# Reordering a planned instruction stream: a later landing time for transposed planes, a preferred sum, a moved row addition (four-layer graph network, one core)

## The chip, the cores and the metric

The kernel runs on one core of one Trainium2 chip. The metric is device time in microseconds (us); lower is better. Three runs of the kernel before took 2829.81, 2833.12 and 2834.18 us, median 2833.12. One further execution was profiled.

In the profile, PE is TensorE's matmul, PEld its weight load, DVE is VectorE, ACT is ScalarE, POOL is GpSimd and SP is SyncE, which only issues DMAs. "out<-in" names what an instruction writes and reads, and "x4" counts instructions.

## The reference

The input x has 128 graphs of 64 nodes with 512 features, float32. Four layers follow one another, each h = relu(layernorm(x)) and then x = x + f(h):

- layers 0, 1 and 3: q, k, v = h Wq, h Wk, h Wv; attention with 8 heads of 64 inside each graph of 64 nodes, masked by one 64 x 64 adjacency matrix, with a softmax; layers 1 and 3 then multiply by an output matrix, and layer 3 also adds a layer norm of the result to it;
- layer 2: rel = (h Wq)(h Wk)^T inside a graph, multiplied by the adjacency matrix, each row divided by its norm, then rel (h Wv), without a softmax.

Every projection is a product of 8192 x 512 by 512 x 512. All arithmetic is in float32.

## The kernel before

**Tiles.** The 8192 rows are cut into 16 tiles of 512 rows (8 graphs), so there are 64 steps n = 0 to 63, layer l = n // 16. A tile of step n is held transposed as `hT`. x lives in DRAM between the layers, one tensor for each of them (`x_0`, `x_1`, ..., `out_dram`).

**Products.** A projection (`projection`, L644) is a Strassen-Winograd product: 7 products of half-size blocks, each one bank of PSUM and 1.73 us of TensorE (8 matmuls of 128x256, started 216 ns apart). Their operands are `hT` itself and `S`, sums of its quarters, or `SO` for the output projections. In layers 1 to 3 one of the seven is cut a second time ("finer"): its 7 small products come as two groups, "4a" and "4b", in the same bank. After 4a, ScalarE copies two quarters (`q<-mm`, z5) and VectorE adds `q` ("u2"); 4b must wait for that. After 4b `close_2` (L633) makes the last quarter of the result on POOL and VectorE. Product 7 ends with the sum "Y22" of `u3` and `z5`, which POOL makes for nearly all projections (`qT<-u,z`, `kT<-u,z`, `v<-u,z`, about 1.3 us each). The order of the seven is a list: `ORDER`, `FINER`, and `LAST_V` for the very last v.

**Planes.** A tile is transposed by DMA (`turn`, L516). VectorE, or ScalarE for the attention's weights, splits the float32 values into two 16-bit planes (`z<-xin`, `z<-s`). SP issues a transposing DMA (`hp<-z`). ScalarE joins the planes (`hT<-hp`, `s<-hp`):

```python
split(zp, src.bitcast(U16).rearrange("p (f w) -> p w f", w=2))
plan.sync.dma_start(
    hp.rearrange("p w c t -> p (w c) t"), zp.rearrange("p w f -> p (w f)"), transpose=True
)
act.copy(dst.bitcast(U16).rearrange("p c (t w) -> p w c t", w=2), hp)
```

POOL then makes `S` from `hT` (`sums_x`, L571). The attention (`attend`, L830) takes the scores (`s<-mm,mask` and the maxima `mx` on VectorE, the shift `s<-s,mx` on POOL), the exponential on ScalarE, the sums `sr` and the scaling, and then transposes `s` in the same way.

**Layer 2.** It has two projections, with the folded weight Wq^T Wk (`a2`) and with Wv (`v2`). `relate` (L1043) makes the relation, its norms `ss` and the factor `rn`, and VectorE's evacuations `xo` of the values use `rn`.

**Additions to x.** `adds` (L1016) adds to a tile of x in DRAM with an accumulating DMA of 1 MB, issued by POOL: either a result, or a constant row (the bias of layer 1, or `bet` of layer 3) spread over the tile (`x<-row`, `out_dram<-row`). The first row of layers 1 and 3 (steps 16 and 48) is put into a queue of generators, which comes forward by one tick with each product of a projection:

```python
if l in (1, 3) and k == 0:
    spawn(adds(n), 16)
```

**The order.** No instruction is issued while this program runs through the layers. `Plan.record` (L95) notes each as a step with its engine, what it depends on, how long it takes (`busy`) and how long after that its result is there (`late`), both from formulas. `Plan.order` (L156) then plays the steps through on a model of the five engines: whichever engine is free next takes, of its ready steps, the one of the lowest rank. The rank is the place in which the step was recorded, less `RUSH` = 100 for a step that reads PSUM and for one in `plan.hot` (the POOL steps of `close_2` are). `Plan.issue` (L229) issues the steps in the order of their planned starts, so every engine gets a fixed sequence, and all instructions have the line L233. On the chip each engine then takes its sequence in order and waits on semaphores. For DMAs the model holds a time `moved` at which SP's transfers are through, and another (`added`) for POOL's:

```python
elif e == "sync":
    moved = max(moved, at + 1400) + late / (170 if calls[0][2].get("transpose") else 280)
    late = moved + 600 - at - busy
```

Times in the model are in ns. One clock of the generators' queue is one product.

Of the kernel before, what the change touches and what calls it, by code (L numbers as in the profile page):

```python
# [46 lines left out]
LAST_V = (1, 6, "4a", 5, 7, "4b", 2, 3)  # L47
# [11 lines left out]
class Plan:  # L59
# [60 lines left out]
    def add(self, eng, calls, reads, writes, busy, late):  # L120
# [8 lines left out]
        if eng == "tensor":  # L129
            self.products.append(i)  # L130
        elif calls[0][0] == "dma_start" and len(self.products) >= AHEAD:
            deps.add(self.products[-AHEAD])
            if eng == "gpsimd":
# [22 lines left out]
    def order(self):  # L156
        n = len(self.steps)
        wait = [0] * n
        users = [[] for _ in range(n)]
        for i, s in enumerate(self.steps):  # L160
            lags = {**self.lags.get(i, {}), **{d: 0.0 for d in s[2]}}
            wait[i] = len(lags)
            for d, lag in lags.items():
                users[d].append((i, lag))


        rank = [
            i - (n if i in self.front else 0)
            - RUSH * (i in self.hot or any(
                v.tensor.name.startswith("mm_") for c in s[1] for v in c[1][1:] if isinstance(v, bass.AP)  # L170
            ))
            for i, s in enumerate(self.steps)
        ]
        ready = [0.0] * n
        free = {e: 0.0 for e in ("tensor", "vector", "scalar", "gpsimd", "sync")}
        added = 0.0
        moved = 0.0
        port = 0.0
        soon = {e: [] for e in free}
        here = {e: [] for e in free}  # L180
        for i in range(n):
            if not wait[i]:
                heapq.heappush(soon[self.steps[i][0]], (0.0, rank[i], i))
        out = []
        while len(out) < n:
            best = None
            for e in free:
                while soon[e] and soon[e][0][0] <= free[e]:
                    heapq.heappush(here[e], heapq.heappop(soon[e])[1:])
                if here[e]:  # L190
                    at = free[e]
                elif soon[e]:
                    at = soon[e][0][0]
                else:
                    continue
                if best is None or at < best[0]:
                    best = (at, e)
            at, e = best
            if not here[e]:
                while soon[e] and soon[e][0][0] <= at:  # L200
                    heapq.heappush(here[e], heapq.heappop(soon[e])[1:])
            i = heapq.heappop(here[e])[1]
            eng, calls, _, busy, late = self.steps[i]
            moves = calls[0][0] == "dma_start"
            if e == "gpsimd":
                busy += max(0.0, port - at)
            if moves and e == "gpsimd":
                moved = max(moved, at) + 8000
                added = max(added + 6000, at + 8500)
                late = added - at - busy  # L210
            elif e == "sync":
                moved = max(moved, at + 1400) + late / (170 if calls[0][2].get("transpose") else 280)
                late = moved + 600 - at - busy
            elif e == "vector" and late == PORT:
                busy += max(0.0, free["gpsimd"] - at)
                port = at + busy
            free[e] = at + busy
            out.append((at, i))
            for u, lag in users[i]:
                same = self.steps[u][0] == e  # L220
                ready[u] = max(ready[u], at + busy - lag + (0.0 if same and not moves else late))
                wait[u] -= 1
                if not wait[u]:
                    heapq.heappush(soon[self.steps[u][0]], (ready[u], rank[u], u))
        self.start = {i: at for at, i in out}
        self.span = max(free.values())
        return [i for _, i in sorted(out)]
# [47 lines left out]
LEVEL2 = {c + l for l in "13" for c in "qkvo"} | {"a2", "v2"}  # L275
RUSH = 100
WARM = 22
AHEAD = 16


# [37 lines left out]
def gnn_stack_kernel(  # L318
# [11 lines left out]
    plan = Plan(nc)  # L330
# [28 lines left out]
    pw = blocks(mm.take("pw"))  # L359
    for i in range(WARM):  # L360
        pe.transpose(pw[:, i % KC, :], ident, ident)
# [40 lines left out]
    def finer(name):  # L402
        return name in LEVEL2
# [123 lines left out]
    def layer_norm(n):  # L527
# [19 lines left out]
        if n == 0:  # L547
            for t in range(NT):
# [7 lines left out]
                if t == 1:  # L556
                    for i in range(WARM // 2):
                        pe.transpose(pw[:, i % KC, :], xins[n][0][:, ts(i % KC, P)], ident)
# [54 lines left out]
    def quarter(t, prod, i, j):  # L613
        u, v = (j, i) if prod is prod_T else (i, j)
        return t[:, u, v * P : (v + 1) * P]
# [11 lines left out]
    def shared_2(prod, q):  # L627


        i, j = (1, 2) if prod is prod_N else (2, 1)  # L630
        return q[:, 0], q[:, i], q[:, j], q[:, 3]
# [12 lines left out]
    def projection(prod, name, xop, nm, emit, order=None):  # L644
        w = W[name]
        order = order or (FINER if finer(name) else ORDER)

        banks, tmp = {}, {}

        def bank(i):  # L650
            banks[i] = mm.take(f"{i}_{nm}")
            return banks[i]

        def tmp_tile(tag):
            tmp[tag] = p1.tile([P, D], F32, tag=tag, name=f"{tag}_{nm}")
            return tmp[tag]

        X = {1: 1, 2: 1, 6: 6, 7: 6, 5: 5, 3: 5, 4: 4, "4a": "4a", "4b": "4a"}
        for i in order:
            home = X[i]  # L660
            first = home == i
            ps = bank(home) if first else banks[home]
            plan.begin()
            if i in BLOCKS:
                prod(ps, w[:, BLOCKS[i]], xop()[i], first)
            else:
                pv = ps.rearrange("p (u v) -> p u v", u=2)
                prod_2(prod, pv, name, xop(), (1, 5, 6, 4) if i == "4a" else (2, 7, 3))
            plan.end()
            if i == 1:  # L670
                act.copy(tmp_tile("s1"), ps)
            elif i == 2:
                emit("Y11", ps)
            elif i == 6:
                dve.tensor_tensor(tmp_tile("u2"), ps, tmp["s1"], ALU.add)
                emit("u2", tmp["u2"])
            elif i == 5:
                emit("z5", ps, tmp_tile("z5"))
            elif i == 7:
                dve.tensor_tensor(tmp_tile("u3"), ps, tmp["s1"], ALU.add)  # L680
                emit("u3", tmp["u3"])
                emit("Y22", tmp["u3"], tmp["z5"])
            elif i == 4:
                emit("Y21", ps, tmp["u3"])
            elif i == 3:
                emit("Y12", ps, tmp["u2"])
            elif i == "4a":
                q = p1.tile([P, 4, P], F32, tag="q", name=f"q_{nm}")
                q0, u2, u3, z5 = shared_2(prod, q)
                act.copy(q0, quarter(pv, prod, 0, 0))  # L690
                dst, base, mid, bias = emit("close")
                if bias is None:
                    act.copy(z5, quarter(pv, prod, 0, 1))
                else:
                    act.activation(z5, quarter(pv, prod, 0, 1), AF.Identity, bias=bias[1])
                dve.tensor_tensor(u2, quarter(pv, prod, 1, 1), q0, ALU.add)
            elif i == "4b":
                dve.tensor_tensor(u3, quarter(pv, prod, 1, 1), q0, ALU.add)
                dve.tensor_tensor(z5, z5, u3, ALU.add)
                if base is None:  # L700
                    t = tmp["u3"]
                    base = t.rearrange("p (u v) -> p u v", u=2)
                    mid = t[:, P : 3 * P].rearrange("p (u v) -> p u v", u=2)
                close_2(prod, pv, q, base, mid, dst, bias)
            if i in (2, 7, 3, 4, "4b"):
                mm.give(f"{home}_{nm}")
            if i != order[-1]:
                yield
# [307 lines left out]
    def adds(n, y=None):  # L1016
        if y is not None:
            add_out(n, y)
        for i in ROWS.get(n, (1,)) if y is not None else (0,):
            add_out(n + i, R["b1" if n < 2 * NB else "bet"].unsqueeze(1).to_broadcast([P, NT, D]))  # L1020
        yield
# [94 lines left out]
    def spawn(gen, delay=0):  # L1116
        heapq.heappush(queue, (clock[0] + delay, count[0], gen))
        count[0] += 1
# [73 lines left out]
    for n in range(N):  # L1192
# [13 lines left out]
        if n == 3 * NB:  # L1206
            spawn(relate(n), 5)
        if l in (1, 3) and k == 0:
            spawn(adds(n), 16)
        if l != 2:  # L1210
            qT = p1.tile([P, KC, T], F32, tag="qT", name=f"qT_{n}")
            q_emit = emit_bias(region_T(qT), (bqc0, bqc1)[l]) if l < 2 else emit_plain(region_T(qT))
# [45 lines left out]
    for t in range(NT):  # L1258
# [14 lines left out]
        at = slice(t, t + 1)  # L1273
# [41 lines left out]
```

## Time and profile before

| | |
|---|---|
| runs | 2829.81, 2833.12, 2834.18 us |
| profiled execution | 2833.51 us, of which its span (first to last instruction) 2831.7 |
| granted TensorE clock, mean | 0.998 |
| PE busy | 2809.0 us (99%), 26787 matmuls |
| VectorE, POOL, ScalarE busy | 67%, 67%, 53% |
| first product that has real input | at 8.04 us |
| layer 1 starts (n = 16), layer 2, layer 3 | near 700, 1560, 2000 us |
| `x<-row` on POOL, 1 MB each | 16, median 13.8 us to landing |
| `hT<-hp` copies on ScalarE | 252 of 1.353 us in the mean |

The page of the profile first gives the busy time of each engine, then groups of instructions. A wait of an engine is put down to the instruction whose semaphore came last. The chain is the path that ended last, followed back from the end of the program; a "DMA" piece in it is a transfer, "issue" is time in which nothing shows that the engine waited for. Matmuls are pipelined: their records overlap (379 ns each, started every 216 ns), so gaps between them are also read from start to start. The timeline lists an engine's instructions with start and duration, and in brackets how long the engine was idle before and for what.

### The profile page before, as it was taken

To read this page: it belongs to the slowest core of one execution; us is meant where nothing else is said; L and a number is where in the kernel's file an instruction comes from. 1 tells how busy PE (TensorE), PEld (TensorE's weight loads), DVE (VectorE), ACT (ScalarE), POOL (GpSimd) and SP (SyncE) were. 2 spreads that over 40 slices of the span, in tenths; PEclk is the share of its full clock that TensorE was granted. 3 is DMA by queue.
4 is the path that set the end of the run, shared out by engine and by line. 5 is a ranking of instruction groups with operands and counts; after the bars stand their busy time and mean duration, and the time that the engine had idled before them with its cause. 6 is when DMAs were issued, how large, how long until landed. Compare 5 with 4: busy or idle time off the path is not lost.

```text
span 2831.7 us, 65612 instructions
## 1 busy us (share of the span) xinstructions
PE 2809.0 (99%) x26787; PEld 2479.2 (88%) x26787; DVE 1885.2 (67%) x3505; ACT 1489.5 (53%) x2111; POOL 1884.1 (67%) x1849
## 2 busy tenths in 40 slices
PE   9999999999999999999999999999999999999998
PEld 8888788888888888888888888888888888888887
DVE  6666566665666656556656665666578778778777
ACT  5566647555564654645644444443545555555552
POOL 6555565557667666576579645556687887777875
PEclk9999999999999999999999999999999999999999
DMA  6666567556355564564565766565545664554644
GB/s 155 138 152 148 125 157 152 120 135 163 75 104 101 114 129 78 104 122 81 113 129 130 177 155 155 142 157 158 107 82 89 108 114 79 119 106 80 126 84 90
DMA packets 634446, 343.55 MB, mean 121 GB/s; under 512 B 484256, under 2 KB 565408, under 8 KB 634144
## 3 DMA queue, kind: packets, MB, share of 16 engines
q1 hardware_dynamic: 600880, 273.30, 42.5%
q0 software_dynamic: 33264, 66.06, 13.9%
q8 instruction: 209, 3.42, 0.5%
q14 instruction: 93, 0.76, 0.1%
HBM read 120.10 MB, written 102.76 MB: 79 GB/s over the span
## 4 chain that ended last, share of the span: by engine, by line
PE 93%; DVE 2%; DMA 2%; ACT 1%; POOL 1%; SPq 1%; issue 1%; POOLq 0%; DVEq 0%; ACTq 0%
PE mm L233 93%; SPq L233 1%; DVE xo L233 1%; DMA hp<-z 1%; POOL rn L233 0%; DMA xin<-x 0%; ACT s L233 0%; DVE z L233 0%; DMA xin<-in_x_dram 0%; DVE st L233 0%; ACT z L233 0%; POOL S L233 0%; ACT hT L233 0%; DVE u L233 0%; DMA xo<-in_x_dram 0%
## 5 line engine op out<-in xcount | busy, mean ns | idle before, releaser
L233 PE MATMUL mm<-S,w 128*128 128x256 f32 x3584 | 820.0, 380 | 0.6 <-DVE xo L233 0.6
L233 PEld LDWEIGHTS mm<-S,w 128*128 128x128 f32 x3584 | 670.2, 190 | 88.2 <-DVE xo L233 1.0
L233 PE MATMUL mm<-hT,w 128*128 128x256 f32 (+1 forms) x3040 | 618.7, 346 | 1.2 <-DVE q L233 1.0
L233 PEld LDWEIGHTS mm<-hT,w 128*128 128x128 f32 x3040 | 517.6, 190 | 62.0 <-DVE q L233 1.4
L233 DVE TENSOR_TENSOR u<-mm,s 128x512 f32<-128x512 f32 x414 | 283.9, 686 | 304.6 <-PE mm L233 224.4
L233 PE MATMUL mm<-w,S 128*128 128x256 f32 x2048 | 479.6, 382 | 0.7 <-issue 0.7
L233 PEld LDWEIGHTS mm<-w,S 128*128 128x128 f32 x2048 | 378.2, 190 | 52.8 <-issue 2.4
L233 ACT COPY hT<-hp 128x1024 uint16<-128x1024 uint16 x252 | 330.7, 1353 | 142.7 <-DMA hp<-z 142.0
L233 PE MATMUL mm<-w,hT 128*128 128x256 f32 (+1 forms) x1696 | 351.1, 347 | 7.3 <-DVE q L233 5.6
L233 PEld LDWEIGHTS mm<-w,hT 128*128 128x128 f32 x1696 | 293.0, 191 | 44.8 <-DVE q L233 9.2
L233 POOL TENSOR_TENSOR qT<-u,z 128x512 f32<-128x512 f32 x64 | 88.0, 1376 | 346.4 <-DVE u L233 329.0
L233 DVE COPY z<-xin 128x1024 uint16<-128x1024 uint16 x252 | 234.2, 950 | 47.2 <-ACT xin L233 39.2
L233 POOL TENSOR_TENSOR S<-hT 128x512 f32<-128x512 f32 x126 | 172.1, 1366 | 115.0 <-ACT hT L233 115.0
L233 ACT COPY s<-hp 128x1024 uint16<-128x1024 uint16 x188 | 243.8, 1350 | 7.1 <-DMA hp<-z 6.2
L233 POOL TENSOR_TENSOR s<-s,mx 128x1024 f32<-128x1024 f32 x96 | 184.9, 1967 | 70.5 <-DVE mx L233 70.5
L233 PE MATMUL mm<-w,SO 128*128 128x256 f32 x992 | 229.2, 379 | 0.0
L233 ACT ACTIVATE xin<-xin,nb,rs 128x512 f32<-128x512 f32 x256 | 195.3, 811 | 56.9 <-DVE nb L233 56.9
L233 ACT COPY s<-mm 128x512 f32<-128x512 f32 x211 | 122.6, 583 | 187.7 <-PE mm L233 109.4
L233 ACT COPY z<-s 128x1024 uint16<-128x1024 uint16 x188 | 189.6, 1047 | 37.0 <-POOL s L233 36.9
L233 PEld LDWEIGHTS mm<-w,SO 128*128 128x128 f32 x992 | 183.9, 190 | 22.6
L233 DVE BATCH_NORM_STATS2 st<-xin 128x6 f32<-128x512 f32 x256 | 171.8, 671 | 37.7 <-DMA xin<-x 18.8
L233 PE MATMUL mm<-w,oT 128*128 128x256 f32 (+1 forms) x994 | 189.6, 334 | 0.7 <-DVE q L233 0.3
(131 smaller groups left out, 4114.8 us busy)
## 6 DMA issues: line engine op xcount, KB each, us to landing
xin<-x SPq DMA_DIRECT2D x128, 256.0 KB, 3.7
xin<-in_x_dram SPq DMA_DIRECT2D x64, 256.0 KB, 3.9
x<-row POOLq DMA_DIRECT2D x16, 1024.0 KB, 13.8
x<-xo POOLq DMA_DIRECT2D x16, 1024.0 KB, 9.5
xin<-out_dram SPq DMA_DIRECT2D x64, 256.0 KB, 6.6
out_dram<-row POOLq DMA_DIRECT2D x16, 1024.0 KB, 16.6
out_dram<-xo POOLq DMA_DIRECT2D x15, 1024.0 KB, 12.4
out_dram<-xo SPq DMA_DIRECT2D x36, 256.0 KB, 2.5
```

The source lines that it names most:

```text
L233: getattr(getattr(self.nc, eng), op)(*a, **k)
```

## The change

Three edits, all of which act on the order alone; the recorded steps are the same.

```diff
@@ Plan.order
             elif e == "sync":
                 moved = max(moved, at + 1400) + late / (170 if calls[0][2].get("transpose") else 280)
-                late = moved + 600 - at - busy
+                late = moved + (MARGIN if calls[0][2].get("transpose") else 600) - at - busy
@@ constants
 RUSH = 100
 WARM = 22
+MARGIN = 2000
 AHEAD = 16
@@ projection, after product 7
                 emit("u3", tmp["u3"])
                 emit("Y22", tmp["u3"], tmp["z5"])
+                if order is not LAST_V:
+                    plan.hot.add(len(plan.steps) - 1)
@@ the loop over n
         if l in (1, 3) and k == 0:
-            spawn(adds(n), 16)
+            spawn(adds(n), 20)
```

In the model, the result of a transposing DMA is there 2000 ns after `moved` instead of 600. The step Y22 gets the rank of the steps that read PSUM, except in the last v. The first row addition of layers 1 and 3 is recorded four products later: at n = 16 POOL's instruction comes behind the shifts of the scores and the closing sums of v (n = 16), where it was behind the closing sums of kT. The planner's new order differs in many other places by a few instructions on each engine.

## The prediction

> **What bounds the kernel now.** I read the busy shares first, then what TensorE waited for, then the chain of waits at the two places that TensorE's idle time pointed to.
>
> ```profile
> PE 2809.0 (99%) x26787; PEld 2479.2 (88%) x26787; DVE 1885.2 (67%) x3505; ACT 1489.5 (53%) x2111; POOL 1884.1 (67%) x1849
> ```
>
> TensorE is busy for 2809.0 of 2831.7 us; no other engine passes 67%. The change adds no product and takes none away, so all it can move is the rest: some 8.0 us until the first real product (the chain has "8.04 377.42 PE mm"), 7.6 us after the last one (PE's work ends at 2824.1), and the waits between. These are few:
>
> ```profile
> PE mm L233 <- DVE q L233: 6.9, 4, 4.6
> PE mm L233 <- ACT xin L233: 2.6, 1, 2.6
> PE mm L233 <- POOL ident masks.py:199: 1.4, 1, 1.4
> PE mm L233 <- DVE s L233: 1.3, 1, 1.3
> ```
>
> The columns are total us, times, longest. The second and third rows are the start. The first holds one wait of 4.6 us; the chain around it reads:
>
> ```profile
> 705.44 2.58 DMA xin<-x
> 708.02 10.63 DMA hp<-z
> 718.65 0.02 issue
> 718.67 0.04 ACT hT L233
> 718.72 1.16 issue
> 719.87 0.42 ACT q L233 x2
> 720.29 0.02 issue
> 720.32 0.30 DVE q L233
> ```
>
> A transposed plane (hp<-z) took 10.63 us to land, where the two before it, issued at 704.11 and 706.07, took some 3.4. ScalarE's next instruction in its order was the copy of this plane, so two small copies of a product (q<-mm), which had nothing to do with the plane, ran behind it; VectorE's sum q and TensorE's "4b" came after them. The timeline shows what slowed the plane and how long ScalarE stood:
>
> ```profile
> 706.67 1.49 POOL L233 DMA_DIRECT2D x<-row  x1
> 718.67 1.33 ACT L233 COPY hT<-hp 128x1024 uint16<-128x1024 uint16 x1 [7.95 <-DMA hp<-z]
> ```
>
> The row is 1 MB, issued 1.35 us before the plane, and it landed 11.2 us later. After the gap the next 7 matmuls start 427 ns apart instead of 216: 7 x 0.211 = 1.48 us more. The place costs 4.60 + 0.16 (the start of the restarted one) + 1.48 = 6.2 us.
>
> The other waits, with what the restart adds, are one of 1.43 us at 1745 (sum s), 1.13 at 1557 and 1.18 at 1603 (q), 0.74 at 1999, 0.5 at 878, 0.3 at 1546, together 5.3; and in layer 2 six of 0.22 us (start to start), 57.1 us apart, from 1660.6 to 1947.8, too short for the view of waits, each of this form in the chain:
>
> ```profile
> 1829.58 1.65 POOL rn L233
> 1831.25 0.57 DVE xo L233 x2
> 1831.83 0.22 issue
> 1832.05 1.26 DVE xo L233 x3
> 1833.31 0.21 DVE q L233
> ```
>
> Five evacuations xo stand ahead of q on VectorE, and TensorE's 4b starts at 1833.56, 0.22 late. (The wait at 1603 is one period ahead of the first of them.)
>
> **What the Trainium skill says.** "DMA: Bandwidth & Descriptors", section "Issuing engines are not separate DMA queues": transfers of all queues run on the same 16 engines and interleave. The trace agrees: SP's plane 3.4 us alone, 10.63 beside POOL's row. "TensorE: Matmul & The Clock Gate", section "What's actually happening": the clock halves after an idle window of about 3.4 us. Agrees: only the 4.60 us gap shows the doubled cadence, 427 ns against 216. The same page, "Architectural detail": ScalarE and VectorE run strictly in order; the chain above is that. "SBUF — State Buffer", section "Who interferes with whom": some VectorE copies and GpSimd's instructions lock each other out for a whole instruction. Agrees: z<-xin takes 0.69 at best, up to 1.76 beside POOL, 0.95 in the mean.
>
> **The change part by part.** It changes only the order in which the recorded steps are issued: every engine keeps its instructions. Durations are from the profiled execution, 2833.51 us: span 2831.7 plus 1.8 around it. The runs' median is 2833.12, so 0.4 less.
>
> 1. *First row moved back (16 to 20 ticks), at n=16 and 48.* On POOL the DMA of n=16 now stands behind the shifts of both halves of the scores (s<-s,mx, 1.9 each) and the three closing sums of v, ahead of the four sums S (1.27 each). By then the four planes of the next tile have been issued on SP. So the plane lands in 3.4 us and the 6.2 us go. What is late next: the DMA's 1.49 us of POOL now stand straight before S. By the durations, the second sum ends near 722.6 on before's clock, and TensorE, no longer held, wants S near 721.4: 1.2 us lost (0 to 2.5). The row now overlaps the planes of the attention (s to hp) in place of those of hT; the last copy s<-hp would come near 729.7, about 0.7 us late for the products of the values (0 to 1.5). And v's own 4b keeps a VectorE with two maxima of 1.21 us about it: 0.2 (0 to 0.5). Net at n=16: -6.2 + 2.1 = -4.1; bounds -6.2 and -1.7. At n=48 (out<-row at 2002) TensorE never waited on planes, and the DMA goes behind the sums of a weight: nothing, 0 to +0.5 if S falls late there too.
>
> 2. *Margin: a transposed plane is taken to land 1.4 us later.* The planner puts small ScalarE work (the q and z5 copies, 0.2 to 0.6 us each) ahead of plane copies of 1.35 us. That shortens chains to TensorE; the price is that hT and S come up to 1.4 us later. The cover is there: S is ready 16 us ahead of its first product in layer 2 (1851.7 against 1868), 20 in layer 3 (2212.7 against 2232.2), the half SO 23. In layer 2 VectorE now has q behind four xo, not five, and POOL has rn ahead of rs: one xo of 0.39 us against a lack of 0.22. Six waits go: -1.3 (-1.3 to 0).
>
> 3. *Last quarter's sum (Y22, POOL, 1.38 us) preferred.* It now passes the quarter sums of S and the shifts of the scores, which then come 1.4 us later; the 16 to 23 us above hide that. POOL at 67% has room. Price nothing, up to +1 for values that wait on a later shift. LAST_V is left out of this, but the order of its products moves: 4b comes one product closer to the end, and the values after it wait on VectorE's and POOL's last sums of v: +0.5 (0 to 0.9) in the tail, the rest of which stays at 21.7 us.
>
> 4. *Everything else moves a little.* Of the 5.3 us of single waits, at least that at 1557 (q behind a z copy of 1.76) has its cause moved: z copies now follow q there. At 1745 the input is late by DMA (7.3 us) and stays. I take -1.0 (-4 to +3, since new ones of about 1 us can arise at any change of layer).
>
> Sum: -4.1 - 1.3 + 0 + 0.5 - 1.0 = -5.9, so 2833.1 - 5.9 = **2827.2 us**.
>
> **The rivals.** 0.2%, about what a measurement here can tell from no change, is 5.7 us.
>
> *A: the wait moves, it doesn't go.* The 1 MB row still needs 11 us somewhere, and POOL's in-order queue now puts it before S and beside the planes of the attention. For it: those planes also pass through ScalarE in order. Against: their products have others to run ahead of them. With the upper bound of step 1 (-1.7), layer 2 (-1.3), and the tail and other waits at +0.5 each: -2.0, 2831.1. If layer 2 too keeps its waits: 2832.4.
>
> *B: slower, since the second halves of the finer products start too soon.* In the new order 4b follows 4a after a single product of 1.73 us in 108 of some 158 places (before 90), the others have 3.46. Within 1.73 us ScalarE must copy q0 and z5 (0.42) and VectorE add q (0.30), with whatever its order puts ahead; one xo group and a z copy (0.95) fill it, as layer 2 shows now at 0.22 a place. At 0.22 x 108 = 23.8 the gain is gone and 18 lost. It decides from (5.9 + 5.7) / 0.22 = 53 of the 108 places on; with 58 it ends at 2827.2 + 12.8 = 2840. For it: VectorE is busy for 7 to 8 tenths in most slices of layer 3, 5 to 6 in earlier ones. Against: of before's 90 such places only the six of layer 2 and some four more waited, and the later plane copies clear ScalarE's way.
>
> *C: the order of the plan is not that of the chip*, so the margin does nothing and only step 1 counts: -4.1 + 0.5 = -3.6, 2829.5.
>
> **How the numbers follow.** The main case 0.72; A 0.08; C 0.04; B 0.16. Within the main case the sum spreads from about -9.5 to -3 (2823.6 to 2830), and I put 5 parts of 8 beyond -5.7, since the 5.3 us of single waits leave more room below than the +3 above: 0.45 of all, and 0.27 short of it. A and C fall within 0.2%, B beyond it. Faster 0.45, same 0.27 + 0.12 = 0.39, slower 0.16. The range reaches down to all single waits and the periodic ones gone, with step 1 at its lower bound (-6.2 - 1.3 - 5.3 + 0.5 = -12.3, so 2821), and up to B's 2840.
>
> **What would show it.** Right: no TensorE gap over 1 us near 720 and no run of 427 ns; hp<-z near 3.4 us for the fourth plane of n=17; the row's DMA after v's sums; waits for q down from 6.9 to under 2 us; no waits in layer 2 of period 57 us; PE's busy time within 2 us of 2809 and the whole gain in gaps. Wrong: a wait on S or s near 722 to 730 of over 3 us; many waits for q of 0.2 to 0.4 us in layers 1 to 3; or a hT copy on ScalarE that still stands behind a plane of 10 us with a q copy after it.

## The result: 2820.52 us, and the profile after

The changed kernel took 2820.52 us (median of five runs, 2818.44 to 2821.14), the kernel before 2832.04 in five runs: ratio 0.9958, 95% interval 0.9944 to 0.9973, so 11.5 us less. The forecast was 2827.2, in a range from 2821 to 2840. The sign was right; the size was about half of what came, and the time lies 0.5 us under the range.

The profiled execution took 2818.44 us, its span 2816.5. The page's busy line, and what TensorE waited for:

```profile
PE 2803.3 (100%) x26787; PEld 2476.3 (88%) x26787; DVE 1885.6 (67%) x3505; ACT 1494.9 (53%) x2111; POOL 1876.9 (67%) x1849
```

```profile
PE mm L233 <- POOL ident masks.py:199: 1.4, 1, 1.4
PE mm L233 <- ACT xin L233: 1.0, 1, 1.0
PE mm L233 <- ACT s L233: 0.7, 1, 0.7
...
PE mm L233 <- DVE q L233: 0.3, 1, 0.3
PE mm L233 <- POOL S L233: 0.2, 1, 0.2
```

The waits for q, 6.9 us before, are 0.3; the largest that are not the start are two of 0.7, one of them for a copy s<-mm of ScalarE that empties a bank. But PE's busy time fell too, by 5.7 us, with the same matmuls. "Busy" hides two things: matmuls at half clock, and the short waits inside a group of small matmuls, since the records overlap.

At n = 16 the timeline of POOL shows the row's DMA in its new place, behind the closing sums of v (the first of them is v's Y22):

```profile
712.94 1.28 POOL L233 TENSOR_TENSOR v<-u,z 128x512 f32<-128x512 f32 x1 [0.61 <-DVE u L233]
714.30 0.73 POOL L233 TENSOR_TENSOR u<-u,q 128x256 f32<-128x256 f32 x1
714.99 0.46 POOL L233 TENSOR_TENSOR v<-u,q 128x128 f32<-128x128 f32 x1
715.39 1.49 POOL L233 DMA_DIRECT2D x<-row  x1
716.42 1.77 POOL L233 TENSOR_TENSOR S<-hT 128x512 f32<-128x512 f32 x1
718.27 1.27 POOL L233 TENSOR_TENSOR S<-S,hT 128x512 f32<-128x512 f32 x1
```

And that of ScalarE its two q copies, ahead of the next planes; no small copy stands behind a late plane:

```profile
708.81 0.58 ACT L233 COPY z<-mm 128x512 f32<-128x512 f32 x1
709.28 0.44 ACT L233 COPY q<-mm 128x128 f32<-128x128 f32 x2
709.60 2.58 ACT L233 COPY hT<-hp 128x1024 uint16<-128x1024 uint16 x2
```

SP issued the last plane of the next tile at 709.58, and it landed within 4.3 us, since its copy starts at 713.89; the row comes 1.5 us after that. Layer 2 has lost its periodic waits: four xo, then q (the timeline of VectorE), and TensorE's 4b at 1820.26 follows the product before it without a gap.

```profile
1818.21 1.66 DVE L233 SCALAR_TENSOR_TENSOR xo<-mm,rn,xo 128x256 f32<-128x256 f32 x4 [1.33 <-POOL rn L233]
1819.79 0.28 DVE L233 TENSOR_TENSOR q<-mm,q 128x128 f32<-128x128 f32 x1
```

**An account by start times.** To see the hidden losses too, I took for each matmul the time from the start of the one before it, less the median for that pair of shapes, and summed what came to over 0.15 us at one place (the evenly repeated slow matmuls of layer 2's norms left out, which are the same in all kernels). In us of one profiled execution each:

| kernel | start | rest of layer 0 | 540 to 700 | n = 16 (700 to 760) | 760 to 1640 | 1640 to 2003 | layer 3 | tail | sum | time less sum |
|---|---|---|---|---|---|---|---|---|---|---|
| before | 5.8 | 0.3 | 2.7 | 6.5 | 3.5 | 4.3 | 1.2 | 1.2 | 25.6 | 2807.9 |
| after | 3.5 | 1.2 | 0 | 1.5 | 0.6 | 1.5 | 0 | 1.4 | 9.7 | 2808.8 |
| row_only | 4.0 | 3.1 | 1.9 | 7.5 | 3.0 | 2.8 | 1.1 | 1.2 | 24.6 | 2808.2 |
| margin_only | 4.5 | 0 | 0 | 6.7 | 0.5 | 1.5 | 4.9 | 5.8 | 23.8 | 2808.2 |
| hot_only | 5.7 | 5.2 | 2.1 | 8.6 | 0.2 | 3.1 | 0.3 | 1.4 | 26.6 | 2807.8 |
| move_dma | 6.1 | 1.5 | 0.2 | 4.1 | 3.5 | 3.8 | 0 | 1.2 | 20.3 | 2808.1 |
| swap_act | 4.6 | 1.2 | 2.5 | 6.3 | 3.5 | 3.8 | 0 | 1.2 | 23.0 | 2808.4 |
| after_dma_back | 3.5 | 4.9 | 0 | 7.2 | 0.6 | 0.3 | 0 | 1.4 | 17.9 | 2808.6 |
| margin_1300 | 6.0 | 0 | 0 | 1.1 | 0.8 | 4.4 | 0 | 1.4 | 13.7 | 2808.9 |
| margin_1700 | 3.5 | 1.9 | 0 | 7.0 | 1.0 | 0.7 | 6.9 | 4.1 | 25.0 | 2810.2 |
| margin_3000 | 3.5 | 2.2 | 0 | 1.0 | 1.4 | 0 | 10.7 | 3.6 | 22.2 | 2808.9 |
| after_dma_later | 5.6 | 1.0 | 0 | 9.7 | 0.6 | 0.6 | 0 | 1.4 | 18.8 | 2808.4 |
| row_24 | 3.8 | 1.6 | 0 | 2.2 | 0.6 | 0.6 | 5.4 | 1.4 | 15.6 | 2809.0 |
| margin_hot_k | 5.8 | 0.2 | 0 | 7.9 | 0 | 0.9 | 30.1 | 3.6 | 48.5 | 2808.2 |

The last column (the profiled execution's time less the sum) stays within 2807.8 to 2810.2, while the times lie 38 us apart: the account leaves little out. Each row is one execution, and parts of it are chance. All kernels begin with the same instructions, yet the first column spans 2.6 us: in the six executions with 5.6 to 6.1 the granted clock was halved at the start, in the eight with 3.5 to 4.6 it was not. Before, row_only, move_dma and swap_act share their order up to n = 16, and lose 2.7, 1.9, 0.2 and 2.5 from 540 to 700; the 1.2 of layer 3 before come in one more of these four. So part of the 15.1 us between the two profiled executions is no effect of the change; the medians, 11.5 us apart, bear the weight.

### The profile page after: what moved, and what is told of

It is laid out like the page before. It is cut to its first block, busy times and chain, and to the rows that moved or that the text cites. A ratio compares the mean times of both kernels' runs of the same rounds, so it can differ in the third digit from the quotient of the medians.

```text
span 2816.5 us, 65510 instructions
## 1 busy us (share of the span) xinstructions
PE 2803.3 (100%) x26787; PEld 2476.3 (88%) x26787; DVE 1885.6 (67%) x3505; ACT 1494.9 (53%) x2111; POOL 1876.9 (67%) x1849
## 4 chain that ended last, share of the span: by engine, by line
PE 96%; DVE 1%; DMA 1%; POOL 1%; SPq 1%; issue 0%; ACT 0%; POOLq 0%; DVEq 0%; ACTq 0%
PE mm L233 96%; SPq L233 1%; DMA xin<-x 0%; DMA xin<-in_x_dram 0%; POOL S L233 0%; DVE st L233 0%; DVE xo L233 0%; DMA hp<-z 0%; POOL xo L233 0%; DVE s L233 0%; DMA xo<-in_x_dram 0%; DVE u L233 0%; DVE z L233 0%; DVE kT L233 0%; DVE mx L233 0%
## 5 line engine op out<-in xcount | busy, mean ns | idle before, releaser
L233 DVE COPY z<-xin 128x1024 uint16<-128x1024 uint16 x252 | 219.1, 886 | 38.1 <-ACT xin L233 33.8
L233 POOL TENSOR_TENSOR S<-hT 128x512 f32<-128x512 f32 x126 | 162.0, 1286 | 65.3 <-ACT hT L233 65.3
L233 ACT ACTIVATE s<-s 128x1024 f32<-128x1024 f32 (+1 forms) x112 | 108.2, 968 | 169.3 <-DVE s L233 92.7
## 6 DMA issues: line engine op xcount, KB each, us to landing
out_dram<-xo POOLq DMA_DIRECT2D x15, 1024.0 KB, 10.6
```

The lines of the kernel that those rows point to most:

```text
L233: getattr(getattr(self.nc, eng), op)(*a, **k)
```

## The experiments

Each was timed in rounds against the kernel before on the same chip. The chips differ from one set of rounds to another, and the kernel before took 2832.04 to 2834.02 us in the median on them, so the ratios compare more closely than the times.

**The edits one at a time.** First the third edit: `spawn(adds(n), 20)` in the kernel before.

> The kernel before with the third edit alone (20 ticks for 16). Its order: TensorE's, ScalarE's and SP's sequences are those of before; on POOL the row's DMA of n=16 keeps its place, only that of n=48 moves by two instructions. Theory 1 (the edit does nothing by itself; the DMA at n=16 was moved by the other two edits together): the gap of 4.6 us at 720 stays, time within 1.5 us of the kernel before. Theory 2 (the prediction's step 1): 4.1 us less.

Measured: 2832.62 us, ratio 1.0002 (0.9994 to 1.0011). The edit alone does nothing, as theory 1 said. Nor does it add anything to the other two: compared instruction by instruction, all three edits give on every engine the sequence that the first two give without it. The DMA's new place is a joint effect of the other two edits on the planner.

Then the margin alone, the first edit:

> The kernel before with MARGIN = 2000 alone. The row's DMA of n=16 keeps its place ahead of the shifts, but ScalarE has the q copies ahead of the third and fourth copy of hT there. Theory 1 (what frees TensorE is the order on ScalarE): no gap of more than 2.5 us near 720, so 3 to 4 us from there, 1.5 from the periodic waits of layer 2, 3 from the waits at 1557, 1603 and 1999: 8 us less, 2824. Theory 2 (the prediction's steps 2 and 4; the gap at 720 needs the DMA moved): 2.3 us less.

Measured: 2831.55 us, ratio 0.9997 (0.9989 to 1.0006). Neither theory. What theory 1 wanted from 540 to 2003 did come: without n = 16 those columns hold 2.0 us where before had 10.5. It was given back, in layer 3 and the tail, 10.7 us against 2.4. The waits of TensorE:

```profile
PE mm L233 <- POOL S L233: 3.1, 1, 3.1
PE mm L233 <- ACT z L233: 2.1, 3, 1.1
...
PE mm L233 <- DVE v L233: 1.9, 1, 1.9
...
PE mm L233 <- DVE kT L233: 1.2, 2, 0.6
```

At n = 16 the wait is no longer for q but for S: ScalarE still stands 6.6 us for a plane there. In layer 3 the scores wait for kT at two places, 1.6 us by the account. The chain at one of them reads:

```profile
2403.38 2.97 POOL SO L233 x2
2406.35 0.41 POOL kT L233
2406.77 0.42 POOL oT L233
2407.19 0.07 issue
2407.26 1.29 POOL oT L233 x3
2408.54 1.23 POOL kT L233
```

Sums SO and their quarters (oT) stand on POOL ahead of the large kT sum of 1.23 us, which is Y22. That is the step that the second edit prefers. The other 9 us have several causes: copies of z behind the copy of a plane, a wait for the maxima mx, and in the tail four waits and the one for v.

The preferred Y22 alone, the second edit:

> The kernel before with the preferred Y22 alone. The row's DMA and the q copies behind the fourth plane stay at n=16. Theory 1: the gap near 720 stays; the slow starts of scores (kT,qT) in layer 0, 1.5 us in all between 583 and 666, go, since kT's sum comes sooner; layer 2's waits stay or change by chance: 1 to 2 us less. Theory 2 (the prediction's step 3): nothing, 0 to +1.

Measured: 2831.53 us, ratio 0.9993 (0.9985 to 1.0001). By the account the single waits from 760 to 1640 go, but n = 16 costs 8.6, and layer 2's periodic waits and the wait at 1999 stay. The gain at kT in layer 0 that theory 1 named did not show with this edit (2.1 us are left there, 0 with the margin; but see above how much of that is chance). This execution also shows one wait of 2.1 us near 154, for a plane of the attention; I did not pursue whether the order makes it.

So -0.7 and -0.7 alone, not told from none, but -11.5 together.

**The DMA by itself.** In the kernel before, one instruction moved after planning: the first row's DMA behind the first shift.

```diff
+    row = next(i for i in seq if plan.steps[i][0] == "gpsimd" and plan.steps[i][1][0][0] == "dma_start")
+    pool = [i for i in seq if plan.steps[i][0] == "gpsimd"]
+    behind = pool[pool.index(row) + 1]
+    seq.remove(row)
+    seq.insert(seq.index(behind) + 1, row)
```

> The kernel before with one instruction moved and nothing else: POOL's first row DMA stands behind the first shift s<-s,mx of n=16, not ahead of it, some 8 us later by the trace. Theory 1 (the DMA that slows the plane is the cause of the 6.2 us): the fourth plane lands in under 5 us, the gap near 720 goes, and the DMA's 1.5 us on POOL cost at most 1.2 us ahead of S: 4 to 6 us less. Theory 2 (the plane is slow for another reason, such as SP's own loads of xin around it): the gap stays over 3 us, and the time with it.

Measured: 2827.38 us, ratio 0.9982 (0.9976 to 0.9989), so 5 us less. That the DMA makes the plane late is shown: ScalarE waits 2.0 us for the fourth plane, where it waited 7.95.

```profile
712.82 1.35 ACT L233 COPY hT<-hp 128x1024 uint16<-128x1024 uint16 x1 [2.02 <-DMA hp<-z]
```

What follows it in the chain was not foreseen by either theory:

```profile
722.40 1.28 POOL hT L233 x3
723.68 3.72 POOL s L233 x2
727.40 1.24 POOL v L233
...
728.66 0.85 ACT z L233 x2
...
729.55 1.65 PE mm L233 x3
```

v's Y22 (727.40) stands behind S, the quarters and two passes over s; ScalarE's z5 copies wait for it in turn, and TensorE waits 2.1 us for the bank, then runs at half clock. With the second edit, Y22 of v comes ahead of S, as the timeline of the changed kernel shows above. So this one traced execution gives only 2.4 us less at n = 16 (6.5 to 4.1); another 2.5 us of it lie from 540 to 700, where the order is that of before. The 5 us rest on the medians, of 21 runs against 49.

**ScalarE's order by itself.** In the kernel before, the fourth hT copy of n = 17 put behind the two q copies.

```diff
+    plane = [i for i in act if name(i) == ["hT", "hp"]][4 * 16 + 3]
+    behind = act[act.index(plane) + 2]
+    seq.remove(plane)
+    seq.insert(seq.index(behind) + 1, plane)
```

> The kernel before with one instruction moved: on ScalarE at n=16 the copy of the fourth slow plane stands behind the two q copies, not ahead of them; POOL's DMA keeps its place. Theory B (ScalarE's order is the cause of the 6.2 us): the gap near 720 goes and nothing takes its place, 5 to 6 us less. Theory A (the late plane itself is needed soon after): the wait for q goes, but a wait on S of 2 to 4 us comes within 8 us of it; 0 to 3 us less, 2830.

Measured: 2832.36 us, ratio 0.9994 (0.9985 to 1.0002). Theory A: the wait for q goes, and a wait of 3.3 us for S comes 2.7 us later in the trace. The chain before had named ScalarE's copy; the cause was the plane.

**The DMA back in the changed kernel.** The same kind of move, the other way: the row's DMA five steps forward, ahead of the shifts.

> The changed kernel with one instruction moved: POOL's first row DMA stands ahead of the first shift s<-s,mx of n=16 again. Everything else is the order of the changed kernel, so ScalarE has the q copies ahead of the late planes. Theory A (the DMA's place is what counts, the 1 MB slows the planes and S comes late whatever ScalarE's order is): a wait of 2 to 3.5 us on S near 717, as with the margin alone, and 4 to 5 us more than the changed kernel: 2825. Theory B (with the q copies ahead, the slow plane is harmless): within 1.5 us of the changed kernel, 2821.

Measured: 2825.93 us, ratio to the kernel before 0.9969 (0.9958 to 0.9981). That is 5.4 more than the changed kernel's 2820.52, but those were other rounds; against the kernel before beside it, it gains 8.1 us where the changed kernel gained 11.5, so 3.4 are lost. Theory A in kind; but TensorE's wait, 4.4 us, is not for S. Its chain:

```profile
711.09 8.12 DMA hp<-z
...
719.22 1.33 ACT hT L233
...
722.33 1.33 ACT hT L233
723.65 0.44 ACT v L233
724.09 0.50 ACT s L233
...
724.63 1.65 PE mm L233 x3
```

A plane takes 8.12 us again, and the copies v<-mm and s<-mm, which empty the banks that TensorE needs, stand behind two hT copies. The q copies had gone ahead, so other small copies are the victims. So 3 to 5 of the 11.5 us are the DMA's place, in either kernel. The table agrees: the eight orders with the DMA in its early place lose 6.3 to 8.6 us at n = 16, five of the six with a later place, from the first shift on, 1.0 to 4.1. The sixth is the next experiment.

**The DMA later still.** In the changed kernel, thirteen instructions later, behind the closing sums of the next q.

> The changed kernel with one instruction moved: POOL's first row DMA stands ten groups later, behind the sums S and the closing sums of the next q. Theory: at n=16 some 1.5 us were left in the changed kernel (values 1.0, S 0.5), the first from planes that run beside the DMA, the second from its 1.5 us on POOL; with the DMA later both go: 1 to 1.5 us less than the changed kernel, 2819.3. Rival: the later place only passes the 11 us on to the next planes (hT of the next tile): 0 to +5 us, 2820.5 to 2825.

Measured: 2820.85 us in the median, ratio to the kernel before 0.9962 (0.9948 to 0.9976); three executions took 2820.0 to 2820.9, two 2826.7 and 2827.2. The profiled one is of the second kind, and its chain is the rival's:

```profile
731.07 14.26 DMA hp<-z
...
745.40 1.34 ACT s L233
...
746.78 1.86 PE mm L233 x33
```

The DMA, issued at 730.51, now meets the planes of the attention, and TensorE waits 5.5 us for the values. There was little to gain: S's 0.5 us did go, but the expectation took the wait of 0.72 us near 717 for one of the values, where it is the one for s<-mm, and it is here too, 0.72 us at 719. The changed kernel's place lies between the two groups of planes.

**Other values.** MARGIN 1300, 1700 and 3000 with the rest of the change.

> All three edits with MARGIN = 1300. On POOL the row's DMA of n=16 then comes later still, behind the closing sums of the next q. If the value only has to be large enough to let the DMA move and the q copies pass (theory: steps, not a slope): as fast as with 2000, 2820 within 2. If every ns of margin counts (theory: a slope between the 600 and the 2000): half the gain, 2826.

> All three edits with MARGIN = 1700. Here the row's DMA of n=16 stands at its old early place, ahead of v's closing sums and of S. Theory A (the DMA's place is worth 5 us whatever else the order is): a wait of 3 to 5 us near 720 to 730, so 2825 to 2827, though 1300 and 2000 both gave 2820 to 2822. Theory C (a margin above some value between 600 and 1300 gives the gain): 2820 to 2822.

> All three edits with MARGIN = 3000. The row's DMA of n=16 stands between the two shifts of the scores. Theory 1 (a plane that lands in some 3.4 us from its issue needs no more than 2000; more only delays hT and S): new waits on S or z of about 1 us in layers 1 and 3, 2823 to 2828. Theory 2 (a margin is only ever cover): 2820 or less.

Measured: 1300 gave 2822.10 us (ratio 0.9956, 0.9943 to 0.9968), 1700 gave 2836.65 (1.0014, 1.0007 to 1.0020), 3000 gave 2831.93 (0.9994, 0.9986 to 1.0002). Not a slope, and not one step either. At 1300 the DMA comes late and n = 16 is clean (1.1), but seven periodic waits of layer 2 are there. At 1700 the DMA is back in its early place: 7.0 us at n = 16, theory A, and 11.0 in layer 3 and the tail that theory A had not counted, so the time is above its 2825 to 2827. At 3000 n = 16 and layer 2's periodic places are clean, and layer 3 loses 10.7 us, 7 of them in seven waits of about 1 us, one in a tile, ahead of products of S. What the value sets is which of several orders comes out.

**24 ticks instead of 20**, all else as changed.

> All three edits with 24 ticks in place of 20. The planner then puts the first row's DMA behind the closing sums of the next q by itself, but the order changes in many other places of layers 1 to 3 too. Theory 1 (only the DMA's place matters at n=16, other changes are small): 2818.5 to 2820.5. Rival (any new order brings new single waits of about 1 us): 2821 to 2826.

Measured: 2826.97 us, ratio 0.9975 (0.9966 to 0.9984): the rival, 1 us above what it said. The profiled execution, at 2824.61, loses 2.2 us at n = 16 and 5.4 in layer 3, 4.3 of it by four waits of 0.9 to 1.4.

**Y22 preferred for k alone.**

```diff
-                if order is not LAST_V:
+                if name[0] == "k":
```

> MARGIN = 2000 and 20 ticks, but Y22 preferred only in the projections k. With the margin alone, layer 3 had new waits of the scores for kT (0.6 us each, kT's Y22 behind the sums SO on POOL) and others of 0.5 to 1.1 us for the banks of z. The row's DMA of n=16 keeps its early place. Theory (kT's Y22 is what the margin made late): the waits on kT go, the 5 us at n=16 stay, and the time is 2825 to 2827. Rival (v's and q's Y22 matter as much, the waits for banks): some 6 us of waits in layer 3 and the tail stay, 2829 to 2831.

Measured: 2856.77 us, ratio 1.0081 (1.0067 to 1.0095), worse than either theory. No wait for kT is left, and n = 16 loses 7.9, as the theory said; but layer 3 loses 30 us. The largest part (16.5 us by the account) is what the rival named, the Y22 of v, which is no longer preferred. The largest row of TensorE's waits, and the chain of one of the six:

```profile
PE mm L233 <- DVE z L233: 11.7, 6, 2.4
```

```profile
2379.33 1.27 POOL out_dram L233
2380.60 3.79 POOL s L233 x2
2384.39 1.23 POOL v L233
```

At all six, v's Y22 stands on POOL behind the row's DMA, a shift and a scaling; VectorE's z and an output product wait for it. The place that loses most, 6.9 us by the account, is another: there a plane is late again. Two lines of POOL's timeline, one of SP's and one of ScalarE's:

```profile
2417.66 1.34 POOL L233 DMA_DIRECT2D out_dram<-xo  x1
2418.52 1.80 POOL L233 DMA_DIRECT2D out_dram<-row  x1
```

```profile
2416.36 4.31 SPq L233 DMA_TRANSPOSE hp<-z  x2
```

```profile
2433.91 1.33 ACT L233 COPY hT<-hp 128x1024 uint16<-128x1024 uint16 x1 [11.32 <-DMA hp<-z]
```

Here the two additions of a tile, 2 MB, are issued while SP issues the last two of its four planes. The last plane takes 15.16 us by the chain, ScalarE stands for 11.3, TensorE for 4.3, and the clock is halved about its end. So the mechanism of n = 16 shows at a second place, but most of the 30 us are not due to it. In the changed kernel the same pair is issued at 2401.98 and 2402.84, after SP is through with all four planes and their loads (2394.17 to 2402.31).

No version that I ran beats the changed kernel; MARGIN 1300 and the DMA thirteen instructions later come level in the median.

## Why the prediction was wrong, point by point

The steps that failed are the sizes of step 4 and, less, of step 2, and a term for layer 0 that was put at nothing; step 1 had its size nearly right and its cause wrong.

- **Step 1, the row moved back: size nearly right, credit wrong.** The sum said -4.1 at n = 16; the account shows 6.5 to 1.5, so -5.0, and the moves of the DMA alone give 3 to 5 by the medians. But the step put this down to the edit of the ticks. row_only shows that edit at nothing. I had read the new place in the new order and not asked which edit made it. Of the costs expected behind it, S is late by 0.24 (expected 1.2), the values and 4b not at all (0.7 and 0.2), and one that was not expected, the bank of s<-mm, takes 0.72.
- **Step 2, the margin: the periodic waits went**, as said: six of 0.22 us, 0.33 each by the account (the next small matmuls of the group are late too), so -2.0 and not -1.3. The cover for hT and S that it named holds for the kernel with both edits. With the margin alone layer 3 and the tail lose 10.7 us. None of the waits there is for S: those for kT (1.6 us) come from POOL's sums ahead of Y22, and the rest was not traced to one cause.
- **Step 3, Y22 "price nothing": right alone (-0.7, not told from none), wrong in the sum.** With a margin of 2000 its worth is to keep step 2's gain and to let the DMA move; at 1700 and 3000 layer 3 and the tail lose 11.0 and 14.3 us in spite of it. The sum added the edits as if they were independent. The tail cost 0.2 more than before by the account, where 0.5 was taken.
- **Step 4 is the term that was mis-sized.** It took -1.0 of 5.3 us of single waits. By the account they fell from 5.9 to 1.9 us, so -4.0, the lower end of its range. The waits at 1557, 1603 and 1999 are gone, all three with the margin alone too; the one at 1745 stayed, as said (1.5, then 1.3). With step 2, 760 to 2003 lost 5.7 us less, against a forecast of 2.3.
- **A term was missing:** the stretch from 540 to 700 in layer 0, mostly scores, lost 0.2 to 2.7 us in four executions of before's order and nothing in any of the orders with the margin. I read the view of waits, which shows 0.2 each for two of them, and not the start times. That (1.8 in the mean of the four), steps 2 and 4 (3.4) and step 1 (0.9) come to about what the forecast lacks (5.6), and bring the time below the range. This also undoes the statement that PE's busy time would stay within 2 us.
- **Rival B** (108 second halves too close) did not come: q's waits are 0.3. **Rival A's** wait on S is real, but it comes with the margin or the swap alone, and at MARGIN 1700. **Rival C**, "the margin does nothing and only step 1 counts", is the opposite of what the runs show: by itself the edit of step 1 does nothing.

## What to carry to other kernels

Where an order comes out of a planner, an edit's effect is not its own text: compare the orders that each edit gives alone before giving one of them the credit, and don't add the edits up. A large DMA on one queue can be the cause of a wait that every view names after a small copy on another engine; moving that one instruction in an otherwise fixed order tells cause from victim, and where the order can be chosen, such a DMA goes behind the small transfers that are waited for. And add up TensorE's losses by start times: the waits view held 14.5 us before, the account by start times 25.6.

## What the runs showed of the hardware that I had not expected

**Planes beside an addition.** A plane of 256 KB that lands in 3.3 us by itself took 8.1, 10.6, 14.3 and 15.2 us beside 1 or 2 MB of additions. The Trainium skill ("DMA: Bandwidth & Descriptors", "Issuing engines are not separate DMA queues") says that transfers of all engines "interleave with each other"; here that has a price of 5 to 12 us. What counts is which was issued first. In the 14 traces, as far as they hold the landing, 15 planes were issued within 4 us behind an addition that was still under way, and took 5.5 to 15.2 us; 183 were issued ahead of one and still under way when it came, and took 3.3 us in the median and 5.2 at most.

**The clock after a gap.** Apart from the end of the kernel, the granted clock was halved for 3.41 us at a time, or twice that, and this after gaps of TensorE well under that length: of the twelve from 2.1 to 2.7 us ten (2.1 in move_dma at 729.55 and in hot_only at 154.45, 2.6 at the start of the kernel before), of the seven from 1.8 to 2.0 us one, and all of over 3 us. The Trainium skill ("TensorE: Matmul & The Clock Gate", "What's actually happening") has an idle window of about 3.4 us; here 2.1 us could be enough. The prediction had taken the 4.60 us gap alone as slow, and the start of the same trace, after 2.59 us, was slow too. At the start the same instructions could so lose up to 2.6 us more or less.
